# A four-layer graph network: mask pieces on one queue into eight buffers, and the first broadcast rows in memory of their own

## The chip, the cores and the metric

The kernel runs on one core of a Trainium2 chip. The metric is the device time of one launch in microseconds (us). The engines in the text are PE (TensorE, matrix products; PEld is its weight load), DVE (VectorE), ACT (ScalarE), POOL (GpSimd) and SP (SyncE, which only issues transfers). All transfers of the core run on 16 DMA engines; SP, ACT and POOL each issue into a queue of their own.

## The reference

Four graph layers run one after the other over N = 3327 nodes with 512 features, each added to its input and normalised over the features. The adjacency `adj` is an int32 matrix of 0 and 1, the same for all layers.

```python
# layers 0, 2 and 3: attention with H = 8, 8, 4 heads
Wh = h @ W                                # split into H heads
e = leaky_relu(f1[i] + f2[j], 0.2)        # f1, f2: two dot products of Wh with a
masked = where(adj > 0, e, -9e15)
attention = softmax(masked, axis=j)
h_prime = attention @ Wh                  # per head; layers 2 and 3: elu of it
# layer 1: mean over the first 64 neighbours of each node
keep = (adj > 0) & (cumsum(adj > 0, axis=1) <= 64)
xj = leaky_relu(mean over keep of X @ W_nb.T + b_nb)
xi = leaky_relu(X @ W_line.T + b_line)
out = xi + where(cnt > 0, xj, 0)
# around each layer
x = layernorm(x + layer(x, adj))
```

## The kernel before

Nodes are padded to 26 tiles of 128 (`NT`); a half (`HALF` = 13 tiles, `IW` = 1664 nodes) is what one attention pass covers as columns i.

**The mask.** The transposed adjacency is read once, in 104 pieces of 128 x 832 int32 (416 KB, `QW` = 832), each into a buffer `raw` (`mask_load`), and turned into an fp8 mask that stays in memory for all layers (`mask_set`, on DVE at L524 or on ACT at L523). `mask_steps` makes a list of steps: step k issues the load of piece k and sets the mask of piece k - lag. The pieces are in the order in which the attention needs them: first both quarters of the first half for all tiles in turn, then the third quarter for all tiles, then the fourth. The first 60 (`EARLY`) are issued in the projection of layer 0, from a pool of four buffers (`p_r`) with a lag of 3, two or three steps per tile, in turn from SP's and ACT's queue. The other 44 are `aside` steps of the attention, one per inner step, from two buffers (`rawp`) with a lag of 1; of those the ACT sets the ones whose number k has k % 5 in (1, 3).

**Projection of layer 0.** For each tile t, `project1` transposes the tile of x (four PE transposes, L253) and sums it (L256), and `project2` for the tile before makes 16 products into two PSUM banks (`pw`, L264); ACT copies the columns f1, f2 (`fc`, L268; `dc`, L265), DVE scales the result into `vt` (L270), and SP stores it to DRAM as `v` (L276). The tile of x is loaded by SP into one of three buffers. After tile 14 (`t == HALF + 1`), `prepare` makes the rows `r` of the first half (L298 to L314; four small stores to DRAM on SP) and `cut` splits columns into bf16 parts (L327 to L341). `mean` makes one more row of v after the last tile.

**Attention.** `attention` calls `unit` for two halves x four groups s of heads (`HS` = 2 heads each in layers 0 and 2, 1 in layer 3). A unit first loads for each of its heads the row `r` of this half, broadcast to 128 partitions (`rb`, L353, 832 KB, on POOL's queue, from a pool of `HS` + 1 buffers). Then for each of 26 tiles j it makes t = max(rb, qc) * mask on DVE (L396), a sigmoid y of t on ACT (L399), the products of t with the tile `vj` of v (`po`, PE L405; `vj` comes by SP, L391) and the denominators from y (`pd`, PE L365). In the first unit of layer 0, `prepare` and `cut` of the second half and the counts for layer 1 (`count_jobs`) run as background steps, in the second the small weight products of layers 2 and 3 (`attend`, PE L919).

**Layers 1 to 3.** Layer 1 (`sage`) projects all tiles into `zs` (two bf16 parts that stay in memory) and `zd`, then sums over the kept neighbours (`acc`, PE L728). Its last products are the start of layer 2, whose projection is done tile by tile as each tile of layer 1 is ready; after it `piece_columns` clears `sden` and `sm` on POOL (L245, L247), `cut` runs on DVE, and the attention of layer 2 begins. `third` does the same as layer 0 for layer 3, without mask pieces.

The order of instructions on each engine is that of the program as a scheduler has placed it; an engine runs its own list in order and waits at each instruction for what it needs. Pools hand out buffers; a pool that opens where another has been closed waits until that memory is free.

Of the kernel before, what the change touches and what calls it, by code (L numbers as in the profile page):

```python
# [7 lines left out]
F32 = mybir.dt.float32  # L8
# [10 lines left out]
P = 128  # L19
# [13 lines left out]
def kernel(  # L33
# [189 lines left out]
    class Layer:  # L223
        def __init__(self, li, H, elu):
            self.li, self.H, self.D, self.elu = li, H, F // H, elu
            self.HS = H // NS
            self.vd = dram.tile([NP, F], F32, name=f"v{li}")
            self.rd = dram.tile([H, NP], F32, name=f"r{li}")

# [29 lines left out]
        def project2(self, pool, bank, wsb, xT, t):  # L259
            H, D = self.H, self.D  # L260
            pw = [bank(e) for e in range(2)]
            for c in range(FC):
                for e in range(2):
                    nc.tensor.matmul(pw[e][:, :FW + H], xT[:, c, :], wsb[:, c, e, :], start=c == 0, stop=c == FC - 1)  # L264
            nc.scalar.activation(self.dc[:, t, :], pw[1][:, FW:FW + H], AF.Exp, scale=ALPHA)  # L265
            vt = pool.tile([P, H, D], F32, name="vt")
            for e in range(2):
                nc.scalar.copy(self.fc[:, t, e * H:(e + 1) * H], pw[e][:, FW:FW + H])  # L268
                hs = slice(e * H // 2, (e + 1) * H // 2)
                nc.vector.tensor_tensor(vt[:, hs, :], pw[e][:, :FW].rearrange("p (h d) -> p h d", d=D),  # L270
                                        self.dc[:, t, hs].rearrange("p (h e) -> p h e", e=1)
                                        .to_broadcast([P, H // 2, D]), op=ALU.mult)
            vv = vt.rearrange("p h d -> p (h d)")
            n = P if t < NT - 1 else LAST
            for a, z in _row_pieces(n):
                nc.sync.dma_start(out=self.vd[t * P + a:t * P + z, :], in_=vv[a:z, :])  # L276


        def mean(self, pool, bank, wsb):
# [62 lines left out]
                                            op0=ALU.mult)  # L342


        def unit(self, pools, half, s, background, aside, final=None, ending=None):
            H, D, HS = self.H, self.D, self.HS
            tp, yp, vp, rp, sp, po_p = pools
            i0 = half * IW
            heads = list(range(s * HS, (s + 1) * HS))
            rb = []  # L350
            for h in heads:
                r_ = rp.tile([P, IW], F32, name="rb")
                nc.gpsimd.dma_start(out=r_, in_=self.rd[h:h + 1, i0:i0 + IW].to_broadcast([P, IW]))  # L353
                rb.append(r_)
            po = [po_p.tile([P, 512], F32, name=f"po{c}") for c in range(4)]
            if s == 0:
                self.pd = [po_p.tile([P, 512], F32, name=f"pd{c}") for c in range(2)]
# [117 lines left out]

        def attention(self, extra=None, aside=(), later=None, final=None, ending=None):
            with tc.tile_pool(name="at_r", bufs=self.HS + 1, reuse_waits="tile") as rp, \
                    tc.tile_pool(name="at_t", bufs=3 * self.HS, reuse_waits="tile") as tp, \  # L480
                    tc.tile_pool(name="at_y", bufs=4 * self.HS - (self.li == 0), reuse_waits="tile") as yp, \
                    tc.tile_pool(name="at_v", bufs=4, reuse_waits="tile") as vp, \
                    tc.tile_pool(name="at_s", bufs=2, reuse_waits="tile") as sp, \
                    tc.tile_pool(name="at_po", bufs=1, space=PSUM, reuse_waits="tile") as po_p:
                pools = (tp, yp, vp, rp, sp, po_p)
                jobs = []
                aside = list(aside)
                for half in range(2):
                    for s in range(NS):
                        if extra:  # L490
# [12 lines left out]
    queue_ = [0]  # L503

    def mask_load(pool, t, q):
        n = P if t < NT - 1 else LAST
        i0 = q * QW
        w_ = min(QW, N - i0)
        raw = pool.tile([P, QW], I32, name="raw")
        queue_[0] ^= 1  # L510
        eng = (nc.sync, nc.scalar)[queue_[0]]
        for a, z in _row_pieces(n):
            eng.dma_start(out=raw[a:z, :w_], in_=adjT[t * P + a:t * P + z, i0:i0 + w_])
        return raw
# [9 lines left out]
        return nc.vector.tensor_scalar(dst, raw[:n, :w_], 0.0, None, op0=ALU.is_gt, saturate=False)  # L524


    def mask_steps(pool, pieces, lag, on_act, pinned):
        held = []

        def step(k):  # L530
            if k < len(pieces):
                held.append(mask_load(pool, *pieces[k]))
            if k >= lag:
                ins = mask_set(held[k - lag], *pieces[k - lag], on_act=(k - lag) in on_act)
                if pinned:
# [40 lines left out]
    def sage(first, first_pool, xin, prev, nxt, wsrc, dst):  # L576
# [3 lines left out]
        with tc.tile_pool(name="sg_z", bufs=1, reuse_waits="tile") as zp, \  # L580
# [11 lines left out]
                carry[b, t] = cy  # L592

            load_carry()
            zs = zp.tile([P, NT, 2, F], BF, name="zs")
            zd = dram.tile([NP, F], BF, name="zd")
            with tc.tile_pool(name="sa_w", bufs=1, reuse_waits="tile") as wp, \
                    tc.tile_pool(name="sa", bufs=2, reuse_waits="tile") as fp, \
# [15 lines left out]
                def step2(xt, xT, t):  # L614
# [6 lines left out]
                    nc.scalar.copy(zs[:, t, 0, :], pz)  # L621
                    r1 = sp.tile([P, F], F32, name="r1")
                    nc.vector.tensor_tensor(r1, pz, zs[:, t, 0, :], op=ALU.subtract)
                    nc.scalar.copy(zs[:, t, 1, :], r1)
                    z3 = sp.tile([P, F], BF, name="z3")
                    nc.vector.tensor_tensor(z3, r1, zs[:, t, 1, :], op=ALU.subtract)
# [19 lines left out]
            with tc.tile_pool(name="sb_w", bufs=1, reuse_waits="tile") as wp, \  # L646
# [71 lines left out]
                for b in range(len(blocks)):  # L718
# [3 lines left out]
                    for s in range(G):  # L722
                        acc = ps.tile([P, F], F32, name="acc", bufs=2)
                        for t in range(NT):
                            if b == 0 and len(kts) < NT:
                                kts.append(kept(0, len(kts)))
                            for c in range(3):
                                nc.tensor.matmul(acc, kts[t][:, s * P:(s + 1) * P],  # L728
                                                 zs[:, t, c, :] if c < 2 else zl[:, t, :],
                                                 start=t == 0 and c == 0, stop=t == NT - 1 and c == 2)  # L730
                            if not last and (len(ahead) < 10 and t % 2 == 1 and b > 0 if s == 0 else
                                             len(ahead) < min(NT, t + 11)):
# [20 lines left out]


    def third(first):
        with tc.tile_pool(name="col3", bufs=1) as cp:
            L3.columns(cp)
            L3.more_columns(cp)
            L3.piece_columns(cp)
            with tc.tile_pool(name="p_w", bufs=1, reuse_waits="tile") as wp, \  # L760
# [12 lines left out]
                for t0 in range(0, NT, 2):  # L773
                    ys, ahead = ahead, finish(fp, x2, L2, t0 + 2, 2) if t0 + 2 < NT else None
                    for s, y in enumerate(ys):
# [14 lines left out]
            with tc.tile_pool(name="f3", bufs=2) as fp, tc.tile_pool(name="f4", bufs=1) as gp:  # L790
# [60 lines left out]
                def final(s, q0, n, pt):  # L851
# [17 lines left out]
                L3.attention(lambda pool, half, s: [lambda: L3.prepare(fp, 1, "xr", 2), lambda: L3.cut(fp, 1, "e", 2)]  # L869
                             if (half, s) == (0, 0) else [], later=later, final=final)  # L870
                cut_ = min(8, HALF)
                for qs in (slice(0, cut_), slice(cut_, HALF)):
# [13 lines left out]

    fin0 = ExitStack()
    f0 = fin0.enter_context(tc.tile_pool(name="fin0", bufs=1, side="right"))
    with tc.tile_pool(name="col0", bufs=1) as cp, tc.tile_pool(name="raw", bufs=2) as rawp:
# [61 lines left out]
        def first_jobs(pool, half, s):  # L951
# [14 lines left out]

        pieces = pieces[EARLY:]
        ends = []
        L0.attention(first_jobs, mask_steps(rawp, pieces, 1, [k for k in range(len(pieces)) if k % 5 in (1, 3)], True),
                     ending=lambda: ends.extend(finish(f0, x, L0, 0, 2, 2)))  # L970

    with tc.tile_pool(name="col2", bufs=1) as cp:
        L2.columns(cp)
        L2.more_columns(cp)
        sage(ends, fin0, x, L0, L2, w2, x2)
        with tc.tile_pool(name="fin2", bufs=1) as f2:
            ends = []
            with tc.tile_pool(name="more2", bufs=1, reuse_waits="tile") as mp:
                L2.piece_columns(mp)
                L2.cut(mp, 0, "pc", 1)  # L980
                L2.attention(lambda pool, half, s: [lambda: L2.prepare(mp, 1, "rr", 1), lambda: L2.cut(mp, 1, "pc", 1)]
                             if (half, s) == (0, 0) else [],
                             ending=lambda: ends.extend(finish(f2, x2, L2, 0, 2, 2)))
            third(ends)
# [46 lines left out]
```

## Time and profile before

| | us |
|---|---|
| median of 3 runs | 3499.28 (3495.52 to 3499.89) |
| profiled execution | 3489.1 |
| its span in the profile | 3486.7 |

The profile page gives these busy times, as a share of the span.

| engine | busy us | share |
|---|---|---|
| PE | 3325.6 | 95% |
| DVE | 2694.9 | 77% |
| ACT | 2396.6 | 69% |
| POOL | 181.2 | 5% |

| group of the profile page | count | busy us | mean ns |
|---|---|---|---|
| DVE t L396, 128 x 1664 | 1040 | 1960.1 | 1947 |
| ACT y L399, 128 x 1664 | 1040 | 1771.7 | 1766 |
| PE po L405, 128 x 448 | 8320 | 1939.5 | 522 |
| PE pw L264, 128 x 264 | 1248 | 299.3 | 395 |
| DVE mask L524, 128 x 832 | 86 | 50.2 | 592 |
| POOL issue of rb L353 | 40 | 21.5 | 539 |

The shares are means over stages with different limits. The first projection takes the first 150 us of the span; the attention of layer 0 runs to 985 us, layer 1 to 1818, layer 2's attention from there to about 2620, layer 3's from 2761. In the profile's rows a name such as "raw<-in_adjT_dram" says that something waits for a transfer or an instruction that writes `raw` from the adjacency in DRAM. "DMA share" in a table of windows is the mean busy share of the 16 DMA engines, the last column what they moved in GB/s, and PEclk the clock that TensorE was granted.

### The profile page before, as it was taken

How to read it: one execution, taken by the hardware profiler on the slowest of the kernel's cores; microseconds unless marked ns; L12 is line 12 of the kernel's file. 1: busy time of each engine (PE TensorE's matmuls, PEld its weight loads, DVE VectorE, ACT ScalarE, POOL GpSimd, SP SyncE). 2: the span in 40 equal slices, each digit the busy share in tenths (PEclk: the TensorE clock that was granted, in tenths of full speed). 3: DMA queues.
4: the chain of work that ended last, by engine and by line, in shares of the span. 5: the costliest groups of instructions: out<-in, count | busy, mean ns of one | idle time of the engine just before them, and what ended most of it. 6: DMA issues, size and time to landing. Idle time of an engine off the chain costs nothing.

```text
span 3486.7 us, 48120 instructions
## 1 busy us (share of the span) xinstructions
PE 3325.6 (95%) x18873; PEld 1701.2 (49%) x18926; DVE 2694.9 (77%) x2759; ACT 2396.6 (69%) x2336; POOL 181.2 (5%) x289
## 2 busy tenths in 40 slices
PE   6899999999989999999998999999998999999997
PEld 5644444444444455555553444444446754555553
DVE  5599999999967644434439999999998756668886
ACT  1388989899953343433428999899998655558885
POOL 1000000000000111111110000000001000000000
PEclk9999999999999999999999999999999999999998
DMA  9535211101133432222221111111116511112211
GB/s 352 179 104 161 67 44 41 54 27 51 37 105 125 131 90 73 70 61 75 73 66 35 48 47 48 47 46 46 29 39 197 183 33 44 40 46 91 81 38 47
DMA packets 208452, 276.65 MB, mean 79 GB/s; under 512 B 19321, under 2 KB 140355, under 8 KB 208228
## 3 DMA queue, kind: packets, MB, share of 16 engines
q1 hardware_dynamic: 173622, 157.37, 14.1%
q0 software_dynamic: 22736, 89.80, 8.3%
q10 hardware_dynamic: 11870, 26.42, 2.4%
q8 instruction: 149, 2.44, 0.3%
q14 instruction: 75, 0.61, 0.1%
HBM read 204.92 MB, written 68.60 MB: 78 GB/s over the span
## 4 chain that ended last, share of the span: by engine, by line
PE 62%; issue 24%; DVE 6%; DMA 5%; ACT 3%; POOL 1%; POOLq 0%; DVEq 0%; SPq 0%; ACTq 0%
PE po L405 34%; PE acc L728 9%; PE pw L264 5%; PE pd L365 5%; DVE t L396 3%; PE pz L617 2%; PE pi L620 2%; DMA raw<-in_adjT_dram 2%; ACT y L399 1%; DMA cy<-ctd 1%; PE pt L429 1%; PE pk L696 1%; PE pt L253 1%; DVE kt L700 1%; PE pe L460 1%
## 5 line engine op out<-in xcount | busy, mean ns | idle before, releaser
L396 DVE SCALAR_TENSOR_TENSOR t<-rb,qc,mask 128x1664 f32<-128x1664 f32 x1040 | 1960.1, 1947 | 200.8 <-PE po L405 158.6
L399 ACT ACTIVATE y<-t,bi,sc 128x1664 fp8e4<-128x1664 f32 x1040 | 1771.7, 1766 | 341.4 <-PE pd L365 317.4
L405 PE MATMUL po<-t,vj 128*64 128x448 f32 (+3 forms) x8320 | 1939.5, 522 | 26.0 <-DVE t L396 24.6
L405 PEld LDWEIGHTS po<-t,vj 128*64 128x64 f32 (+1 forms) x8320 | 857.8, 148 | 977.7 <-issue 681.1
L728 PE MATMUL acc<-zs,kt 128*128 128x512 bf16 x1314 | 396.6, 381 | 1.9 <-issue 0.4
L264 PE MATMUL pw<-wsb,xT 128*128 128x264 f32 (+1 forms) x1248 | 299.3, 395 | 21.7 <-DVE vt L270 19.5
L688 ACT CAST pk<-cy 128x256 f32<-128x256 bf16 x338 | 124.0, 374 | 272.7 <-DVE kt L700 224.8
L728 PEld LDWEIGHTS <-kt 128*128 128x128 fp8e4 x2028 | 198.8, 98 | 229.6 <-issue 34.5
L264 PEld LDWEIGHTS pw<-wsb,xT 128*128 128x128 f32 x1248 | 238.9, 196 | 65.6 <-issue 18.8
L365 PE MATMUL pd<-y,sden 128*32 128x448 fp8e4 (+1 forms) x4160 | 259.8, 342 | 10.5 <-ACT y L399 10.5
L700 DVE SCALAR_TENSOR_TENSOR kt<-pk,mask 128x256 fp8e4<-128x256 f32 x338 | 140.9, 421 | 159.5 <-PE pk L696 158.9
L728 PE MATMUL acc<-zl,kt 128*128 128x512 bf16 x661 | 252.1, 381 | 1.1 <-DMA zl<-zd 0.5
L365 PEld LDWEIGHTS <-sden 128*32 128x32 bf16 x4160 | 117.8, 96 | 162.4 <-issue 139.8
L270 DVE TENSOR_TENSOR vt<-pw,dc 128x256 f32<-128x256 f32 x156 | 59.1, 418 | 98.1 <-ACT dc L265 93.5
L696 PE MATMUL pk<-mask,upto 128*128 128x256 fp8e4 x338 | 92.5, 274 | 21.1 <-ACT pk L688 20.0
L353 POOL DMA_DIRECT2D rb<-r x40 | 21.5, 539 | 1646.8 <-DVE t L396 1610.1
L268 ACT COPY fc<-pw 128x8 f32<-128x8 f32 (+1 forms) x156 | 22.8, 163 | 112.1 <-PE pw L264 101.8
L617 PE MATMUL pz<-wn,xT 128*128 128x512 f32 x208 | 95.0, 600 | 1.2 <-ACT xT L611 1.2
L620 PE MATMUL pi<-wl,xT 128*128 128x512 f32 x208 | 93.5, 592 | 0.0
L590 POOL DMA_DIRECT2D cy<-ctd x91 | 67.8, 745 | 400.2 <-ACT pk L688 273.5
L708 DVE SCALAR_TENSOR_TENSOR y<-acc,cnt,bnb 128x512 f32<-128x512 f32 x26 | 19.5, 751 | 85.1 <-PE acc L728 85.1
L524 DVE TENSOR_SCALAR mask<-raw 128x832 fp8e4<-128x832 int32 (+2 forms) x86 | 50.2, 592 | 45.0 <-DMA raw<-in_adjT_dram 44.4
(165 smaller groups left out, 1732.2 us busy)
## 6 DMA issues: line engine op xcount, KB each, us to landing
vj<-v SPq DMA_DIRECT2D x312, 128.0 KB
rb<-r POOLq DMA_DIRECT2D x40, 832.0 KB, 4.7
cy<-ctd POOLq DMA_DIRECT2D x78, 256.0 KB, 3.9
v<-vt SPq DMA_DIRECT2D x75, 256.0 KB
h<-hd SPq DMA_DIRECT2D x65, 256.0 KB
raw<-in_adjT_dram ACTq DMA_DIRECT2D x38, 416.0 KB
raw<-in_adjT_dram SPq DMA_DIRECT2D x37, 416.0 KB
hd<-hb SPq DMA_DIRECT2D x60, 256.0 KB
```

The lines of the kernel that those rows point to most:

```text
L264: nc.tensor.matmul(pw[e][:, :FW + H], xT[:, c, :], wsb[:, c, e, :], start=c == 0, stop=c == FC - 1)
L365: nc.tensor.matmul(pd[c][32 * kk:32 * kk + 32, :w_], lhsT, rhs, start=(kk, c) not in seen, skip_group_check=final is not None, stop=last a ...
L396: nc.vector.scalar_tensor_tensor(t, rb[k], self.qc[:, j, h:h + 1], mask[:, j, i0:i0 + IW], op0=ALU.max, op1=ALU.mult)
L399: nc.scalar.activation(y, t, AF.Sigmoid, bias=self.bi[:, j, h:h + 1], scale=self.sc[:, j, h:h + 1], saturate=False)
L405: nc.tensor.matmul(po[c][k * D:(k + 1) * D, :z - a_], vj[:, j % 2, k * D:(k + 1) * D], ts[k][:, a_:z], start=j == 0, stop=j == NT - 1)
L590: nc.gpsimd.dma_start(out=cy[:, :n, :], in_=ctd[t:t + n, b * GW:(b + 1) * GW] .rearrange("(o t) i -> o t i", o=1).to_broadcast([P, n, GW]))
L617: nc.tensor.matmul(pz, xT[:, c, :], wn[:, c, :], start=c == 0, stop=c == FC - 1)
L620: nc.tensor.matmul(pi, xT[:, c, :], wl[:, c, :], start=c == 0, stop=c == FC - 1)
L688: nc.scalar.copy(pks[k % 2], carry[b, t // 4 * 4][:, t % 4, :])
L696: nc.tensor.matmul(pk, upto, mask[:, t, i0:i0 + GW], start=False, stop=True, skip_group_check=True)
L700: nc.vector.scalar_tensor_tensor(kt, pk, NEIGHBOURS, mask[:, t, i0:i0 + GW], op0=ALU.is_le, op1=ALU.mult, saturate=False)
L728: nc.tensor.matmul(acc, kts[t][:, s * P:(s + 1) * P], zs[:, t, c, :] if c < 2 else zl[:, t, :], start=t == 0 and c == 0, stop=t == NT - 1 ...
```

## The change

There are four parts.

1. **Mask pieces.** `mask_load` takes its queue as an argument. The first four pieces go out on ACT's queue, all others on SP's, in the projection and in the attention. The early pool has 8 buffers in place of 4 and a lag of 5 in place of 3; 3 or 4 steps are issued per tile in place of 2 or 3; and `EARLY` is 88 in place of 60, so that 16 pieces are left for the attention.
2. **Transfers of the first projection.** The stores of v in layer 0 and the loads of x from tile 3 on are issued by POOL in place of SP.
3. **First rows.** The loads of `rb` become a method `rows`. For the first unit of each attention they are issued ahead of it: in layers 0 and 3 after `prepare` at tile 14 of the projection, in layer 2 ahead of `piece_columns`. The pool of the rows is opened outside of `attention`, so that it does not share memory with what runs before. Its number of buffers is the same as before (3, 3 and 2).
4. **Layout.** `zs` becomes two tiles of 13 node tiles each, and the pool `fin2` is placed on the other side of the memory.

```diff
-                nc.sync.dma_start(out=self.vd[t * P + a:t * P + z, :], in_=vv[a:z, :])
+                (nc.gpsimd if self.li == 0 else nc.sync).dma_start(out=self.vd[t * P + a:t * P + z, :], in_=vv[a:z, :])
...
+        def rows(self, rp, half, s):
+            rb = []
+            for h in range(s * self.HS, (s + 1) * self.HS):
+                r_ = rp.tile([P, IW], F32, name="rb")
+                nc.gpsimd.dma_start(out=r_, in_=self.rd[h:h + 1, half * IW:(half + 1) * IW].to_broadcast([P, IW]))
+                rb.append(r_)
+            return rb
...
-            rb = []
-            for h in heads:
-                r_ = rp.tile([P, IW], F32, name="rb")
-                nc.gpsimd.dma_start(out=r_, in_=self.rd[h:h + 1, i0:i0 + IW].to_broadcast([P, IW]))
-                rb.append(r_)
+            rb, self.first_rows = self.first_rows or self.rows(rp, half, s), None
...
-            with tc.tile_pool(name="at_r", bufs=self.HS + 1, reuse_waits="tile") as rp, \
-                    tc.tile_pool(name="at_t", bufs=3 * self.HS, reuse_waits="tile") as tp, \
+            with tc.tile_pool(name="at_t", bufs=3 * self.HS, reuse_waits="tile") as tp, \
...
-    queue_ = [0]
-
-    def mask_load(pool, t, q):
+    def mask_load(pool, t, q, eng):
...
-        queue_[0] ^= 1
-        eng = (nc.sync, nc.scalar)[queue_[0]]
...
-                held.append(mask_load(pool, *pieces[k]))
+                held.append(mask_load(pool, *pieces[k], nc.scalar if k < ahead else nc.sync))
...
-            zs = zp.tile([P, NT, 2, F], BF, name="zs")
+            zs_ = [zp.tile([P, HALF, 2, F], BF, name=f"zs{i}") for i in range(2)]
...
+        with tc.tile_pool(name="col3", bufs=1) as cp, tc.tile_pool(name="at_r3", bufs=2, reuse_waits="tile") as rp:
...
                             L3.prepare(pp, 0)
+                            L3.first_rows = L3.rows(rp, 0, 0)
                             L3.cut(pp, 0)
...
+    with tc.tile_pool(name="col0", bufs=1) as cp, tc.tile_pool(name="raw", bufs=2) as rawp, \
+            tc.tile_pool(name="at_r0", bufs=3, reuse_waits="tile") as rp:
...
-                tc.tile_pool(name="p_r", bufs=4, reuse_waits="tile") as rw0, \
+                tc.tile_pool(name="p_r", bufs=8, reuse_waits="tile") as rw0, \
...
-            EARLY = 2 * NT + 8
-            msteps = mask_steps(rw0, pieces[:EARLY], 3, (), False)
+            EARLY = 3 * NT + 10
+            msteps = mask_steps(rw0, pieces[:EARLY], 5, (), False, 4)
...
-                load_tile(xt, x, t, nc.sync)
+                load_tile(xt, x, t, nc.sync if t < 3 else nc.gpsimd)
...
-                for _ in range(3 if t % 5 < 2 else 2):
+                for _ in range(3 + t % 2):
...
                     L0.prepare(pp, 0)
+                    L0.first_rows = L0.rows(rp, 0, 0)
                     L0.cut(pp, 0)
...
-        with tc.tile_pool(name="fin2", bufs=1) as f2:
+        with tc.tile_pool(name="fin2", bufs=1, side="right") as f2:
             ends = []
-            with tc.tile_pool(name="more2", bufs=1, reuse_waits="tile") as mp:
+            with tc.tile_pool(name="at_r2", bufs=3, reuse_waits="tile") as rp, \
+                    tc.tile_pool(name="more2", bufs=1, reuse_waits="tile") as mp:
+                L2.first_rows = L2.rows(rp, 0, 0)
                 L2.piece_columns(mp)
```

More of the change, by code (lines that the diff above doesn't have):

```diff
@@ L226, in __init__ @@
             self.HS = H // NS
+            self.first_rows = None
             self.vd = dram.tile([NP, F], F32, name=f"v{li}")
@@ L473, in unit, with attention @@
             return jobs[:2] + [reciprocals] + jobs[2:]
-        def attention(self, extra=None, aside=(), later=None, final=None, ending=None):
-            with tc.tile_pool(name="at_r", bufs=self.HS + 1, reuse_waits="tile") as rp, \
-                    tc.tile_pool(name="at_t", bufs=3 * self.HS, reuse_waits="tile") as tp, \
+        def attention(self, rp, extra=None, aside=(), later=None, final=None, ending=None):
+            with tc.tile_pool(name="at_t", bufs=3 * self.HS, reuse_waits="tile") as tp, \
                     tc.tile_pool(name="at_y", bufs=4 * self.HS - (self.li == 0), reuse_waits="tile") as yp, \
@@ L524, in mask_set, with mask_steps @@
         return nc.vector.tensor_scalar(dst, raw[:n, :w_], 0.0, None, op0=ALU.is_gt, saturate=False)
-    def mask_steps(pool, pieces, lag, on_act, pinned):
+    def mask_steps(pool, pieces, lag, on_act, pinned, ahead=0):
         held = []
@@ L594, in sage, with zs @@
             load_carry()
-            zs = zp.tile([P, NT, 2, F], BF, name="zs")
+            zs_ = [zp.tile([P, HALF, 2, F], BF, name=f"zs{i}") for i in range(2)]
+            def zs(t, c):
+                return zs_[t // HALF][:, t % HALF, c, :]
             zd = dram.tile([NP, F], BF, name="zd")
@@ L620, in step2 @@
                         nc.tensor.matmul(pi, xT[:, c, :], wl[:, c, :], start=c == 0, stop=c == FC - 1)
-                    nc.scalar.copy(zs[:, t, 0, :], pz)
+                    nc.scalar.copy(zs(t, 0), pz)
                     r1 = sp.tile([P, F], F32, name="r1")
-                    nc.vector.tensor_tensor(r1, pz, zs[:, t, 0, :], op=ALU.subtract)
-                    nc.scalar.copy(zs[:, t, 1, :], r1)
+                    nc.vector.tensor_tensor(r1, pz, zs(t, 0), op=ALU.subtract)
+                    nc.scalar.copy(zs(t, 1), r1)
                     z3 = sp.tile([P, F], BF, name="z3")
-                    nc.vector.tensor_tensor(z3, r1, zs[:, t, 1, :], op=ALU.subtract)
+                    nc.vector.tensor_tensor(z3, r1, zs(t, 1), op=ALU.subtract)
                     nc.sync.dma_start(out=zd[t * P:(t + 1) * P, :], in_=z3)
@@ L728, in sage @@
                                 nc.tensor.matmul(acc, kts[t][:, s * P:(s + 1) * P],
-                                                 zs[:, t, c, :] if c < 2 else zl[:, t, :],
+                                                 zs(t, c) if c < 2 else zl[:, t, :],
                                                  start=t == 0 and c == 0, stop=t == NT - 1 and c == 2)
@@ L755, in third @@
     def third(first):
-        with tc.tile_pool(name="col3", bufs=1) as cp:
+        with tc.tile_pool(name="col3", bufs=1) as cp, tc.tile_pool(name="at_r3", bufs=2, reuse_waits="tile") as rp:
             L3.columns(cp)
@@ L867, in final @@
                             nc.vector.bn_aggr(out=mv[:, q, :], in_=st[:, q, :, :])
-                L3.attention(lambda pool, half, s: [lambda: L3.prepare(fp, 1, "xr", 2), lambda: L3.cut(fp, 1, "e", 2)]
+                L3.attention(rp, lambda pool, half, s: [lambda: L3.prepare(fp, 1, "xr", 2), lambda: L3.cut(fp, 1, "e", 2)]
                              if (half, s) == (0, 0) else [], later=later, final=final)
@@ L888 @@
     f0 = fin0.enter_context(tc.tile_pool(name="fin0", bufs=1, side="right"))
-    with tc.tile_pool(name="col0", bufs=1) as cp, tc.tile_pool(name="raw", bufs=2) as rawp:
+    with tc.tile_pool(name="col0", bufs=1) as cp, tc.tile_pool(name="raw", bufs=2) as rawp, \
+            tc.tile_pool(name="at_r0", bufs=3, reuse_waits="tile") as rp:
         L0.more_columns(cp)
@@ L968 @@
         ends = []
-        L0.attention(first_jobs, mask_steps(rawp, pieces, 1, [k for k in range(len(pieces)) if k % 5 in (1, 3)], True),
+        L0.attention(rp, first_jobs, mask_steps(rawp, pieces, 1, [k for k in range(len(pieces)) if k % 5 in (1, 3)], True),
                      ending=lambda: ends.extend(finish(f0, x, L0, 0, 2, 2)))
@@ L975 @@
         sage(ends, fin0, x, L0, L2, w2, x2)
-        with tc.tile_pool(name="fin2", bufs=1) as f2:
+        with tc.tile_pool(name="fin2", bufs=1, side="right") as f2:
             ends = []
-            with tc.tile_pool(name="more2", bufs=1, reuse_waits="tile") as mp:
+            with tc.tile_pool(name="at_r2", bufs=3, reuse_waits="tile") as rp, \
+                    tc.tile_pool(name="more2", bufs=1, reuse_waits="tile") as mp:
+                L2.first_rows = L2.rows(rp, 0, 0)
                 L2.piece_columns(mp)
                 L2.cut(mp, 0, "pc", 1)
-                L2.attention(lambda pool, half, s: [lambda: L2.prepare(mp, 1, "rr", 1), lambda: L2.cut(mp, 1, "pc", 1)]
+                L2.attention(rp, lambda pool, half, s: [lambda: L2.prepare(mp, 1, "rr", 1), lambda: L2.cut(mp, 1, "pc", 1)]
                              if (half, s) == (0, 0) else [],
```

## The prediction

> **What bounds the kernel now.** I read the windows of equal stages first, to see which resource is full in each stage, then the chain of waits inside the first projection and at the start of each attention, then shorter windows and the timeline for the bounds.
>
> ```profile
> core 0: us, PE busy (x) PEld busy (x) DVE busy (x) ACT busy (x) POOL busy (x), PEclk, DMA share, GB/s
> 0.00:100.00 100.00, 70.89 (x314) 59.34 (x315) 54.68 (x107) 13.72 (x57) 12.66 (x26) 0.97 0.99 350
> 100.00:164.00 64.00, 54.85 (x271) 45.42 (x269) 32.87 (x91) 17.82 (x61) 2.37 (x4) 0.95 0.47 159
> 164.00:273.00 109.00, 101.54 (x744) 42.93 (x745) 105.50 (x75) 90.01 (x61) 0.34 (x1) 0.97 0.37 108
> 273.00:384.00 111.00, 104.30 (x754) 50.82 (x750) 104.84 (x69) 95.89 (x68) 1.58 (x4) 0.97 0.45 134
> ...
> 489.00:587.00 98.00, 96.68 (x675) 43.79 (x673) 97.32 (x54) 91.03 (x61) 1.06 (x2) 1.00 0.14 44
> ```
>
> For 100 us the DMA engines are full (share 0.99) while TensorE (PE) is busy 71%: the projection is bound by bytes. From 100 to 164 us the DMA engines are half empty (0.47). In attention units 0 and 1 (164 to 273, 273 to 384) VectorE (DVE) is 97% and 94% busy and each takes 109 and 111 us, against 98 us for unit 3 (last line), which sets no mask and is 99% DVE. So there is free DMA time before the attention, and masks cost time inside it.
>
> ```profile
> 27.45 0.60 DVE mask L524
> 28.05 0.02 issue
> 28.07 6.43 DMA raw<-in_adjT_dram
> ...
> 35.15 6.33 DMA raw<-in_adjT_dram
> ```
>
> This is the chain in the projection (start, length, what): each tile stops 6 us for a `raw` piece, not for a computation. And where the attention starts:
>
> ```profile
> 156.16 0.58 issue
> 156.74 6.63 DMA rb<-r
> 163.37 0.03 issue
> 163.39 1.96 DVE t L396
> ```
>
> The chain there is the load of the broadcast rows `rb`. DVE has other work meanwhile: its idle time before the first two `t` is 2.51 and 0.69 us in the timeline, so the 6.63 us are mostly covered. At the two other attentions:
>
> ```profile
> 1823.97 0.04 DVE pc L327
> ...
> 1824.10 0.51 DVE vt L270
> 1824.62 0.03 DVE rest L328
> 1824.64 7.20 DMA v<-vt
> ...
> 2756.64 4.50 PE pw L264 x21
> 2761.14 1.87 DVE t L396
> ```
>
> In layer 2 a 7.20 us store wait leads, in layer 3 the last projection matmuls: neither start is set by `rb`.
>
> **The change, part by part.** One profiled execution gives the durations: it took 3489.1 us (span 3486.7). The median shown is 3499.28 us, 1.0029 times as much; I make the sum against 3489.1 and scale the result by 1.0029.
>
> (a) *Start of the first attention: +1.5 us, bounds -5.2 and +12.8.* Of the 104 pieces, 88 instead of 60 now come before the attention. A piece is 128 x 832 x 4 B = 0.426 MB, so 28 more are 11.9 MB. Before, 100 x 0.350 + 64 x 0.159 = 45.2 MB moved up to 164 us, of which two pieces for the attention (0.85 MB) and four `vj` loads of 0.128 MB (0.5 MB) will now come later. That leaves 45.2 - 1.35 + 11.9 = 55.8 MB before the last early piece. At the 350 GB/s of the full window, 159.4 us. Per tile that is 3.5 pieces plus a 0.26 MB load of x and store of v, 2.02 MB or 5.8 us, against 4.0 us of PE (`pw` x16 3.56 plus `pt` 0.44) and 3.6 us of DVE (3.5 x 0.594 + 2 x 0.42 + 0.69): DMA sets the pace to the last tile, and the cover for the extra sets is the DVE's own waiting. After the last piece come its set (0.6 us) and, in the changed order of DVE, seven small instructions of the second `cut` (about 3 us), then two `t` of 1.95: 159.4 + 0.6 + 3.0 + 3.9 = 166.9. Before, the second `t` ended at 163.39 + 1.96 = 165.35. The `rb` wait is gone from this, since its three 0.85 MB loads are inside the 55.8 MB (they were inside the 45.2 MB too). The bounds are the slowest and fastest ten microseconds with DMA full:
>
> ```profile
> 20.00:30.00 10.00, 10.00 (x42) 8.46 (x42) 6.12 (x13) 1.48 (x5) 0.00 (x0) 1.00 0.99 327
> ...
> 70.00:80.00 10.00, 5.88 (x30) 4.73 (x29) 6.32 (x14) 1.85 (x9) 0.00 (x0) 1.00 1.03 385
> ```
>
> At 327 GB/s the last piece is there at 170.6, +12.8 in the end. At 385 it is there at 145, and then the old chain decides without its `rb` step: 156.2 + 3.9 = 160.1, -5.2.
>
> The Trainium skill ("DMA: Bandwidth & Descriptors", Specifications) gives about 358 GB/s as the limit of memory for one core; the trace has 353, 373 and 385 over ten microseconds, so the row decides. By the page alone the last piece would be there at 156 us and this term would be -2.
>
> (b) *Fewer mask sets in units 0 and 1: -9.4 us, bounds -9.5 and 0.* Of the 44 late pieces DVE set 26 and ACT 18; of the 16 left, DVE sets 10 and ACT 6. All 16 fall in unit 0. So unit 0 loses 6 x 0.59 = 3.5 us of DVE and unit 1 10 x 0.59 = 5.9. DVE is the full engine there, so both count. ACT's 12 sets of 0.976 us count for nothing: it is busy 90 of 109 us. Zero is the bound if PE (101.5 and 104.3 us busy) holds the units up instead. The sets that move into the projection cost nothing there, as (a) counts them under the DMA pace; without that cover, 16.6 us of DVE (28 x 0.592).
>
> (c) *Waits for transfers in units 0 and 1: -2 us.* The chain has 4.90 us for `raw` at 253.31, 4.47 for `wt` at 327.49 and 3.30 for `wt` at 354.29. The first happens in unit 0, where pieces stay; the others stand beside 10 pieces that leave, but a `wt` load also waits for its one buffer, and that stays. PE's busy time is the floor: 109 + 111 - 101.5 - 104.3 = 14.2 us is all that (b) and (c) can give together. The other bound is 0.
>
> (d) *Layer 2: +2 us, bounds 0 and +5.8.* The rows are issued before the memsets, but did not lead. What changes is DVE's order: the first `cut` ran from 1823.97 to 1829.8 while the projection's last stores landed, and is now queued behind `rc`, which needs the last tile's `fc` (1830.65). So 5.8 us of DVE leave an idle gap and fall where `t` starts. In return `t` goes ahead of the second `cut`: the first `t` moves only from 1837.51 to 1838.8 (+1.3), and DVE has 2.08 us of waiting soon after (at 1855.26) that absorbs part. I take +2.
>
> (e) *Layer 3: -1.5 us, bounds -4 and +1.* With rows already there, `t` goes one tile earlier in DVE's order and the first sigmoids too. The start before holds a PE stall from the `x21` group's end at 2761.14 to 2776.56 with table switches of 1.28 us each on ACT; a tile (4.0 us) is the most that can come forward, one switch the most that is lost.
>
> (f) *At nothing.* The queue moves: 25 v stores and 23 x loads now issue on POOL at 0.53 us each, 25 us of an engine that is idle from 20 to 100 us; the cover is that idleness, and the price without it 1.1 us a tile. Behind POOL's wait for the `r` rows stand the stores and x loads of two to three tiles; x is loaded two tiles ahead (11.5 us), and the `r` write stands behind at most eight pieces (8 x 0.426 / 0.350 = 9.7 us), so PE just about keeps x. SP's `vj` loads now wait for the end of the projection, two microseconds while the first `t` run. The split `zs` changes nothing: its first cast waits for its own matmul (1012.4).
>
> One sentence of the same page, in "SWDGE vs HWDGE vs iDMA", speaks against the move to POOL: the software queue's rings lie in on-chip memory that DVE can lock POOL out of. The trace has the `rb` issues at 0.528 us in 480 to 600 us with DVE 99% busy, as fast as elsewhere, and I add nothing; the page gives no time for a sum.
>
> Sum: 1.5 - 9.4 - 2 + 2 - 1.5 = -9.4 us; 3479.7, times 1.0029 = **3490 us**.
>
> **Rivals.**
>
> *1. The projection grows by more than the units shrink (slower).* Its place is the DMA engines from 100 us on, where `rb`, x and v sit on one queue and all `raw` on another, and POOL's stalls let bytes run dry. The trace's own sign is the stretch in which early pieces mixed with `r` traffic:
>
> ```profile
> 95.00:110.00 15.00, 14.51 (x68) 11.70 (x69) 11.74 (x37) 4.77 (x18) 0.00 (x0) 0.89 0.91 309
> ```
>
> At 309 GB/s over all 55.8 MB the last piece is there at 180.6: (a) becomes +22.7 and the sum +11.8, so 3511 us. Against it: PE was full in that stretch, so the demand had ended. It decides from 317 GB/s down (last piece at 176 us); between 331 and 317 the sum is 0 to 0.2%.
>
> *2. More than the sum (faster).* The DMA engines hold 373 to 385, the start comes at its floor (-5.2), and the units fall to PE's busy time (-14.2): with d and e as above -18.9, so 3480 us. For it: two of eight windows reach it. Against: 350 is the mean of all.
>
> *3. The sets that leave are replaced by other idle time, no change.* PE or the counts that hang on the last pieces hold units 0 and 1: (b) is 0 and the sum 0, 3499 us. For it: unit 4 takes 103 us without mask sets, so not all of the excess is masks. Against: DVE busy 105.5 of 109.
>
> **How the numbers follow.** About 0.2% (7 us) is what can be told from no change. Forecast 3490, own range 3483 to 3497: 0.40 (faster 0.27, same 0.13). Rival 1: 0.25 (slower 0.22, same 0.03). Rival 2: 0.20, all faster. Rival 3: 0.15 (same 0.10, slower 0.05). Faster 0.47, same 0.26, slower 0.27. The low end is the floors of (a), (b), (c) and (e) with (d) at 0: -5.2 - 14.2 - 4 = -23.4, 3476; the high end rival 1, 3511.
>
> **What would show it.** (a): DMA share near 1 to about 160 us, and the second `t` ending near 167; later than 175 and rival 1 is true. (b): units 0 and 1 near 105 and 103 us. (c): the `wt` waits shorter. (d): `cut` behind `rc`, first `t` 1.3 us later after the last `acc`. (e): PE's stall before the long `po` run shorter by 1 to 2 us. A projection with DMA share below 0.9 before its last tile would break the pace of (a) and the forecast with it.

## The result and the profile after

| | before | after |
|---|---|---|
| median | 3497.4 us (4 runs, 3491.38 to 3499.89) | 3477.0 us (4 runs, 3474.25 to 3483.24) |
| ratio | 1 | 0.9947 (95% interval 0.9927 to 0.9966) |
| profiled execution | 3489.1 us | 3476.2 us |

The change makes the kernel 0.5% faster. The medians differ by 20.4 us, the two profiled executions by 12.9. What follows compares profiled executions, at points that both have in their timelines. The "second `t`" is the second of the DVE instructions `t` with which the attention begins. "Rows of unit n" is the `rb` load that POOL issues when the last `t` of unit n - 1 with its first head frees a buffer, and so marks the end of unit n - 1.

| us | before | after | difference |
|---|---|---|---|
| end of the second `t` | 165.35 | 159.81 | -5.5 |
| rows of unit 1 | 272.66 | 266.99 | -5.7 |
| rows of unit 2 | 383.69 | 367.21 | -16.5 |
| rows of unit 7, layer 0 | 886.36 | 869.93 | -16.4 |
| last `y` of layer 1 | 1818.07 | 1799.61 | -18.5 |
| rows of unit 7, layer 2 | 2528.44 | 2512.71 | -15.7 |
| end of the last DVE instruction | 3478.21 | 3464.83 | -13.4 |

All of the gain is there when unit 2 of layer 0 begins. The windows of the changed kernel, with the same columns as those of the prediction (span, then busy time of PE, PEld, DVE, ACT and POOL, the granted clock, DMA share, GB/s):

```profile
0.00:100.00 100.00, 83.95 (x412) 72.00 (x413) 63.00 (x136) 20.90 (x80) 35.09 (x61) 1.00 0.99 370
100.00:164.00 64.00, 45.01 (x185) 33.86 (x184) 43.56 (x91) 14.59 (x41) 11.87 (x20) 0.84 0.85 319
```

The DMA engines are as full as before in the first 100 us (0.99), but move 370 GB/s in place of 350, and PE is busy 84 us in place of 71. From 100 to 164 us they are now used, 0.85 in place of 0.47. Between 20 and 80 us the difference is larger:

```profile
20.00:80.00 60.00, 46.81 (x211) 38.53 (x211) 34.67 (x69) 8.09 (x38) 0.00 (x0) 0.97 1.00 355
```

is the kernel before, and

```profile
20.00:80.00 60.00, 57.71 (x280) 49.38 (x281) 40.51 (x80) 12.56 (x50) 17.74 (x28) 1.00 1.03 404
```

the changed one: 404 GB/s, and PE busy 57.7 of 60 us. The DMA engines are full there too, but PE's waits for DVE's `vt` in this stretch fall from 13.2 to 2.3 us: it hardly stops any more. DVE's timeline at the start of the attention in the changed kernel (start, length, line, what, and in brackets the idle time before it):

```profile
155.79 0.37 DVE L342 TENSOR_SCALAR sm<-pc 128x156 bf16<-128x156 bf16 x1
156.01 7.52 DVE L402 SCALAR_TENSOR_TENSOR t<-rb,qc,mask 128x1664 f32<-128x1664 f32 x4
...
175.16 5.68 DVE L402 SCALAR_TENSOR_TENSOR t<-rb,qc,mask 128x1664 f32<-128x1664 f32 x3 [3.47 <-PE po L411]
```

`t` follows `cut` without a gap: no wait for rows. The gap of 3.47 us for `po` comes later; the kernel before has one of 2.92 us at 179.44, there put down to ACT's `y`. The clock granted to PE is 0.58 in 156 to 166 us and 0.50 in 160.7 to 170.7 before. Unit 1, before and then after:

```profile
272.60:383.60 111.00, 104.30 (x750) 51.04 (x750) 104.84 (x69) 95.89 (x67) 1.61 (x3) 0.97 0.45 134
```

```profile
267.00:367.20 100.20, 99.92 (x755) 47.47 (x751) 98.04 (x56) 88.18 (x58) 1.65 (x3) 1.00 0.20 63
```

DVE has 6.8 us less work (13 set instructions, 7.7 us, are gone), and its idle time falls from 6.2 to 2.2 us; PE is now full. The chain's waits for `wt` (weights that `attend` reads), 4.47 and 3.30 us before, are gone from it; what is left of PE's waits for `wt` is 0.6 us each.

### The profile page after: what moved, and what is told of

The parts are those of the page before. It is cut to its first block, busy times and chain, and to the rows that moved or that the text cites. A ratio compares the mean times of both kernels' runs of the same rounds, so it can differ in the third digit from the quotient of the medians.

```text
span 3474.4 us, 48117 instructions
## 1 busy us (share of the span) xinstructions
PE 3320.6 (96%) x18873; PEld 1700.4 (49%) x18926; DVE 2699.8 (78%) x2771; ACT 2387.0 (69%) x2324; POOL 213.3 (6%) x340
## 4 chain that ended last, share of the span: by engine, by line
PE 59%; issue 27%; DVE 6%; DMA 5%; ACT 2%; POOL 1%; ACTq 0%; POOLq 0%; SPq 0%; DVEq 0%
PE po L411 33%; PE acc L734 9%; PE pd L371 4%; PE pw L265 4%; DVE t L402 3%; DMA raw<-in_adjT_dram 3%; PE pz L623 3%; PE pi L626 2%; PE pt L435 1%; ACT y L405 1%; DMA cy<-ctd 1%; PE pk L702 1%; DVE kt L706 1%; PE pe L466 1%; PE pt L254 1%
## 5 line engine op out<-in xcount | busy, mean ns | idle before, releaser
L526 DVE TENSOR_SCALAR mask<-raw 128x832 fp8e4<-128x832 int32 (+2 forms) x98 | 58.4, 603 | 51.0 <-DMA raw<-in_adjT_dram 50.7
```

## The experiments

Times within a kernel are from its profile. The same table serves all of them; ratios are against the kernel before, on the same chip. "Per busy time" is the rate over 20 to 80 us divided by the DMA share. Each row is one execution; the stretch from unit 2 to unit 7, whose code is the same in all, takes 501.2 to 503.4 us, so differences of two or three microseconds between rows are not read.

| kernel | GB/s, share, per busy time | first `t` | rows of unit 1 | of unit 2 | of unit 7 | ratio |
|---|---|---|---|---|---|---|
| before | 355, 1.00, 355 | 160.75 | 272.66 | 383.69 | 886.36 | 1 |
| after | 404, 1.03, 392 | 156.01 | 266.99 | 367.21 | 869.93 | 0.9947 (0.9927-0.9966) |
| 1: x, v on SP | 304, 0.87, 349 | 194.57 | 304.11 | 404.30 | 905.80 | 1.0063 (1.0048-1.0078) |
| 2: pieces on two queues | 394, 1.03, 383 | 175.19 | 284.71 | 385.06 | 887.10 | 0.9999 (0.9989-1.0008) |
| 3: four buffers | 372, 1.00, 372 | 164.33 | 276.46 | 376.81 | 879.18 | 0.9984 (0.9973-0.9996) |
| 4: before, 88 early | 350, 0.99, 354 | 176.11 | 286.81 | 387.22 | 888.79 | 0.9997 (0.9987-1.0006) |
| 5: no rows ahead | 406, 1.03, 394 | 150.24 | 260.47 | 360.78 | 863.09 | 0.9938 (0.9916-0.9960) |
| 6: rows ahead in layer 0 only, r on ACT | 407, 1.03, 395 | 153.10 | 263.34 | 363.50 | 865.96 | 0.9937 (0.9920-0.9954) |
| 7: x, v on ACT | 381, 1.01, 377 | 157.19 | 267.50 | 367.57 | 869.89 | 0.9950 (0.9936-0.9965) |
| 8: 60 early | 400, 1.03, 388 | 144.38 | 256.13 | 363.36 | 865.22 | 0.9946 (0.9929-0.9962) |
| 9: 60 early, no rows ahead | 402, 1.03, 390 | 145.21 | 259.29 | 368.61 | 869.79 | 0.9939 (0.9923-0.9956) |
| 10: no rows ahead, r on ACT | 406, 1.03, 394 | 151.50 | 261.92 | 362.33 | 865.75 | 0.9933 (0.9920-0.9947) |
| 11: as 10, 74 early | 407, 1.03, 395 | 144.06 | 257.44 | 362.66 | 864.58 | 0.9938 (0.9925-0.9950) |
| 12: before, queues alone | 357, 0.97, 368 | 151.13 | 264.39 | 374.32 | 877.00 | 0.9977 (0.9965-0.9988) |

**1 to 4: which part raises the rate.** The profile after had shown more bytes per busy microsecond, which no step of the prediction holds. Three parts of the change could be the cause; one run takes back each, and the fourth makes the other half of the change alone.

Run 1, on the changed kernel:

```diff
-                (nc.gpsimd if self.li == 0 else nc.sync).dma_start(out=self.vd[...], in_=vv[a:z, :])
+                nc.sync.dma_start(out=self.vd[...], in_=vv[a:z, :])
-                load_tile(xt, x, t, nc.sync if t < 3 else nc.gpsimd)
+                load_tile(xt, x, t, nc.sync)
```

> The changed kernel with the x loads and the layer-0 v stores back on SP. Theory A (packets): the transfers of x and v are what made the DMA engines faster, since on POOL's queue they go in packets of about 4 KB and on SP's of 2 KB; the rate over 20 to 80 us falls from 404 to about 355 GB/s, the first t moves from 156.0 to 165-172 us, and the time rises by 10 to 15 us to 3487-3492. Rival B (one queue for the pieces) and rival C (eight buffers): the rate stays near 404, the first t stays within 4 us of 156, the time within 5 us of 3477.

It was far worse than either theory: slower than the kernel before (1.0063), first `t` 38.6 us later than in the changed kernel. The rate per busy time falls to 349, as theory A said, but the DMA engines are also idle for 13% of the time, which nobody had forecast. The chain of waits in this run:

```profile
70.54 0.33 SPq L277
70.87 0.04 issue
70.91 0.51 SPq L515
71.42 0.06 issue
71.48 1.52 SPq L515
73.00 0.04 issue
73.04 0.02 SPq L126
73.06 0.05 issue
73.11 4.68 DMA xt<-in_x_dram
```

SP issues a store of v (L277), then pieces (L515), and only then the load of x (L126) that PE waits for. What holds SP up is the store, which waits until DVE has made `vt`. SP's largest group of waits in 20 to 190 us (us in total, times, longest):

```profile
SPq L277 <- DVE vt L271: 89.0, 24, 9.9
```

With two smaller entries, SP stood 98.4 us at the stores of v, and 2.0 us at the pieces. PE waited 41.2 us for `xt` in the same time. The pieces stand behind the same stores, which fits the DMA engines running dry.

Run 2, on the changed kernel:

```diff
-                held.append(mask_load(pool, *pieces[k], nc.scalar if k < ahead else nc.sync))
+                held.append(mask_load(pool, *pieces[k], nc.scalar if k < ahead or k % 2 else nc.sync))
```

> The changed kernel with every second piece on ACT's queue again (x and v stay on POOL's, eight buffers). Theory A: the rate over 20 to 80 us stays at 395 GB/s or more and the time within 5 us of 3477, apart from what ACT loses by waiting at its own issues. Rival B: the rate falls to about 355 GB/s, the first t comes at 165-172 us, the time is 3487-3492.

The rate stays at 394 GB/s, so rival B falls: one queue for the pieces does not make the DMA engines faster. Yet the first `t` is 19 us later, and 17 us remain at unit 7. What is left of the theory is "what ACT loses by waiting". ACT's waits in 20 to 150 us (engine and line, for what; us in total, times, longest), first in the kernel before:

```profile
ACT dc L265 <- DVE mask L524: 43.4, 10, 6.2
ACT fc L268 <- PE pw L264: 24.9, 11, 3.4
```

then in the changed kernel, where no wait for `mask` is among them (the two longest),

```profile
ACT fc L269 <- PE pw L265: 75.1, 24, 9.4
ACT xT L256 <- PE pt L254: 17.1, 23, 12.0
```

and in run 2:

```profile
ACT dc L266 <- DVE mask L526: 28.4, 8, 5.0
...
ACT fc L269 <- DVE mask L526: 14.3, 3, 5.0
ACT xT L256 <- DVE mask L526: 10.1, 4, 2.8
```

`dc` reads nothing that a mask set writes. It waits because ACT stands at the issue of a piece ahead of it, and that piece waits until DVE has emptied its buffer. In the kernel before, ACT's timeline has the issue and, right behind it, `dc` after 5.41 us of idle time:

```profile
57.75 0.34 ACTq L513 DMA_DIRECT2D raw<-in_adjT_dram  x1
58.13 0.18 ACT L265 ACTIVATE dc<-pw 128x8 f32<-128x8 f32 x1 [5.41 <-DVE mask L524]
```

As DVE's `vt` needs `dc`, and PE needs the bank that `vt` frees, the whole tile then goes at the pace of the pieces. With the pieces on SP (all but the first four), ACT waits for no mask set, and 98.6 of its 110.9 us of waiting are for PE.

Run 3, on the changed kernel: `bufs=8` of the early pool back to 4, and the lag from 5 to 3.

> The changed kernel with 4 buffers and a lag of 3 for the early pieces. Theory A: the rate over 20 to 80 us stays at 390 GB/s or more; only the stretch around the r writes (80 to 100 us) loses a little more, the first t comes 0 to 6 us later, time 3477-3483. Rival C: with four pieces in flight the rate falls to about 355 GB/s, the first t comes at 165-172 us, the time is 3487-3492.

Between the two: 372 GB/s over 20 to 80 us, and unit 7 9.3 us later. Eight buffers (with the longer lag that goes with them) matter, and not only around the r writes.

Run 4, on the kernel before: `EARLY = 3 * NT + 10`, and `3 + t % 2` steps per tile.

> The kernel before with 88 early pieces and 3.5 of them per tile, nothing else changed. All theories: the rate stays at about 355 GB/s, so the last early set comes at 160-168 us and the rows are loaded behind it; the second t ends at 170-178 us in place of 165.4, unit 1 falls by about 10 us, and the time is 3493-3501. If the number of early pieces alone were the gain, it would be 3480-3487.

As expected by all, the rate is 350 GB/s and unit 1 10.6 us shorter. The second `t` ends at 180.9 us, 2.9 us beyond the forecast's range. The later start and the shorter unit cancel (0.9997). Moving 28 pieces is worth nothing at the rate of the kernel before.

**5 to 8: the rows, the r writes, the kind of queue, the number of pieces.** Run 5, on the changed kernel (and likewise in layers 2 and 3, with the pool opened in `attention` as before):

```diff
-                    L0.first_rows = L0.rows(rp, 0, 0)
...
-        L0.attention(rp, ...
+        L0.attention(None, ...
```

> The changed kernel with all three pools of the rows inside the attention again and no rows issued ahead; queues, buffers and early pieces stay. Read by stage. Layer 0: if the rows of their own memory are worth something, the first t waits for rows that are issued only when the projection's memory is free, and starts 3 to 8 us later than 156.0 (rival: nothing, as the rows were hidden behind other work before, at most 2 us). Layer 2: from the last y of layer 1 (L714 in the changed kernel) to the first row load of unit 1 it took 117.7 before and 119.9 after; theory: 117.7 again (rival: 119.9, if something else of the change costs it). Layer 3: the projection is 4 to 8 us faster without the rows' transfers among its own, and the attention's start 4 us slower; net 0 to 4 us faster.

The expectation for layer 0 had the wrong sign: the first `t` comes 5.8 us earlier without the rows ahead. DVE's timeline shows the wait that they avoid:

```profile
150.24 1.95 DVE L402 SCALAR_TENSOR_TENSOR t<-rb,qc,mask 128x1664 f32<-128x1664 f32 x1 [1.95 <-DMA rb<-r]
152.74 13.13 DVE L402 SCALAR_TENSOR_TENSOR t<-rb,qc,mask 128x1664 f32<-128x1664 f32 x7 [0.55 <-DMA rb<-r]
```

2.5 us of idle time. What they cost stands in the windows of 100 to 140 us, first with rows ahead (the changed kernel), then without (this run):

```profile
100.00:140.00 40.00, 30.46 (x133) 24.66 (x132) 21.87 (x44) 6.63 (x27) 9.00 (x15) 0.91 1.03 388
```

```profile
100.00:140.00 40.00, 36.06 (x168) 29.56 (x168) 26.95 (x57) 7.14 (x32) 10.04 (x15) 1.00 1.03 392
```

The DMA engines are full in both, and PE gets through 168 matrix instructions in place of 133. The rows are 2.56 MB, 6.2 us at 410 GB/s, which other transfers of a stage that is bound by bytes then lack; that this is what they cost is argued from these windows, and runs 8 and 9 below fit it. The sum is -5.1 us for the end of the second `t` (154.69 against 159.81). In layer 2 neither number of the expectation came: from the last `y` to the rows of unit 1 it took 121.0 us, but 116.8 in runs 10 and 11, which have the same layer 2, so this stretch tells nothing of the rows; layer 3 is told of below.

Run 6 keeps the rows ahead in layer 0 alone, and issues the r writes of the first half by ACT:

```diff
-                nc.sync.dma_start(out=self.rd[...], in_=rr[:, :n * P])
+                (nc.scalar if self.li == 0 and half == 0 else nc.sync).dma_start(out=self.rd[...], in_=rr[:, :n * P])
```

> The changed kernel with the rows of layers 2 and 3 as before the change, and the four r writes of the first half of layer 0 issued on ACT's queue in place of SP's. Theory: SP stood behind those writes, so that the rate fell to 311 GB/s in 80 to 100 us; now it is 380 or more there, and the first t comes at 151-155 in place of 156.0. Layers 2 and 3 gain 2 and 0 to 4 us. Time 3468-3475. Rival: the fall of the rate comes from the row and r traffic itself; then the first t stays at 156 and the time is 3472-3477.

The rate in 80 to 100 us rises from 311 to 372 GB/s, and the first `t` comes 2.9 us earlier: part of that stretch's fall was SP standing behind the writes. The rate of 380 that the theory had was not reached. The time, 3469.9 us, is in the theory's range and below the rival's, but the kernel before took 3492.0 us there in place of 3497.4, so the time does not separate them.

Run 7, on the changed kernel: `nc.gpsimd` becomes `nc.scalar` in the two lines that run 1's diff takes away.

> The changed kernel with the x loads and v stores of layer 0 on ACT's queue in place of POOL's. It tells packets from order. Theory A (packets): on a hardware queue of their own the transfers of x and v still go in 2 KB packets, and the bytes per busy time of the DMA engines stay at about 350 GB/s over 20 to 80 us (rate divided by busy share), as with x and v on SP. Rival D (a queue of their own, no matter of which kind): 385 GB/s or more. Time: under A 3485-3495, under D 3475-3485, since ACT waits at its own stores.

Run 7 settles theory A, which run 1 could not. In 40 to 80 us x and v go in packets of 1.8 KB on average on ACT's queue (2418 packets for 4.43 MB) against 3.3 KB on POOL's (1517 for 4.97 MB), and the rate there is 408 GB/s against 412. Over 20 to 80 us it is 381 GB/s (377 per busy time), below the forecast of rival D, because it starts slowly (356 in 20 to 50 us, 406 in 50 to 80). So small packets are not the cause. With x and v on a queue without pieces all runs with eight buffers have 377 to 395 GB/s per busy time, and those with four 368 to 372; with x and v among the pieces it is 349 with eight and 354 to 355 with four. That the mixture itself makes the DMA engines slower is not shown. In run 1 SP also stood at the stores of v, so that less may have been under way, and the kernel before, with its mixed queue and four buffers, reaches the rate of the changed one for eight microseconds:

```profile
64.00:72.00 8.00, 6.63 (x32) 5.37 (x30) 4.35 (x9) 1.59 (x8) 0.00 (x0) 0.93 1.04 412
```

In turn the changed kernel falls to 311 GB/s at a share of 0.94 in 80 to 100 us, 331 per busy time, with its queues as they are. What sets the bytes per busy time stays open.

Run 8: `EARLY = 2 * NT + 8` in the changed kernel.

> The changed kernel with 60 early pieces in place of 88. Theory: the projection is no longer short of bytes, the first t comes at 147-152 us (PE's own time plus the tail), but units 0 and 1 take 111 us each as in the kernel before; so 9 to 11 us are lost in unit 1 and 4 to 9 won at the start: 3475-3485. If the early pieces are the whole gain, 3490-3497.

It is as fast as the changed kernel (0.9946 against 0.9947) with none of the 28 pieces moved, so they are not the gain. The first `t`, at 144.4 us, is 11.6 us earlier and earlier than forecast; unit 1 is only 7.0 us longer (107.2 us against 100.2; 111.0 before).

**9 to 12: combinations.** Run 9 is run 5 with 60 pieces, run 10 run 5 with run 6's r writes, run 11 the same with 74 pieces; run 12 is the kernel before with the two lines of the changed kernel that run 1's diff takes away, and `eng = nc.sync` for every piece.

> The changed kernel with 60 early pieces and no rows issued ahead in any layer. In the run without rows the start of the attention was bound by bytes and won 3.3 us by leaving the rows out; in the run with 60 pieces it was bound by TensorE. Theory: with 60 pieces the rows ahead are worth something, because nothing else stands in the way: the first t comes 1 to 4 us later than the 144.4 of the run with 60 pieces and rows, the rows of unit 7 are issued at 862-868, and the time is 3467-3474, no better than without rows at 88. Rival: rows ahead cost in any case (POOL's queue waits for them); first t at 140-144, unit 7 at 857-862, time 3462-3467.

Run 9: the first `t` is 0.8 us later where 1 to 4 were forecast, unit 7 1.8 us beyond its range, the time (3473.46) inside. At 60 pieces, where bytes no longer bind (DMA share 0.54 in 100 to 140 us of run 8), leaving the rows out costs 4.6 us at unit 7; at 88 it saves 6.8. Of the 4.6 us only 0.8 are there at the first `t`, and the rest, in units 0 and 1, is not explained. The rival's start and unit 7 did not come. The ratios, over the whole kernel, don't separate the two (0.9939 and 0.9946).

> The changed kernel without rows issued ahead, and with the r writes of the first half of layer 0 on ACT's queue. Theory: both gains add, as one is fewer bytes and one a stall of SP's queue: the rate in 80 to 100 us is 400 or more in place of 333, the first t comes at 146-149 in place of 150.2, unit 7's rows at 859-862, time 3464-3468. Rival: TensorE is the bound by then (it is busy 1.00 up to 140 us in the run without rows), and nothing more comes: unit 7 at 863, time as in the run without rows.

Run 10: the theory falls, with 357 GB/s in 80 to 100 us, first `t` at 151.5, unit 7 at 865.75. The two gains don't add. Against run 6, which has the r writes on ACT and the rows ahead, leaving the rows out brings 1.6 us at the first `t` and 0.2 at unit 7, so the 6.8 us of run 5 are not the price of the rows alone.

> As the run before in this list, with 74 early pieces. Theory: 14 pieces fewer take 6.0 MB or 15 us off the DMA engines, so the start is TensorE's: first t at 143-147; 14 pieces in units 0 and 1 cost 8 of them on DVE, 5 us. The two cancel: unit 7's rows at 858-863, within 3 us of the run with 88. Rival: the start does not move (it is TensorE's already at 88), so 74 loses 3-6 us.

Run 11: the start is PE's, as forecast (144.06), and unit 7 comes within 1.2 us of run 10, though both later than expected.

> The kernel before with two edits alone: the x loads and v stores of layer 0 on POOL's queue, all pieces on SP's. Four buffers, a lag of 3, 60 pieces and the rows stay as before. Theory: the queues are most of the gain, since ACT no longer waits at pieces' issues and SP's queue is no longer mixed: the projection's tiles take less than 5 us, the last early set comes by 95-100 us in place of 110.6, the first t by 150-156 in place of 160.8, time 3480-3488. Rival: without the eight buffers nothing comes (four buffers cost 9.3 us at unit 7 in the changed kernel): time 3488-3495.

Run 12 lies in between: 0.9977, first `t` at 151.1, unit 7 9.4 us earlier than before. The sets did not all come as early as forecast (three stand at 107 to 109 us). The queues alone give a good half of the 16.4 us at unit 7; the rest comes only with the other parts, of which the buffers (run 3, 9.3 us) are the one whose own run shows a gain there.

No version is shown to be faster than the changed kernel. Run 10 has the lowest ratio, 0.9933 (0.9920 to 0.9947), and the intervals of runs 5 to 11 all overlap with that of the changed kernel (0.9927 to 0.9966). At unit 7 of the profiles run 5 is 6.8 us ahead.

## Why the prediction was half right

The sign was right. The time, 3477.0 us, lies below the forecast's own range (3483 to 3497) and 1 us inside the whole range, whose low end was 3476. The size, -9.4 us in the sum, was -13.4 at the end of DVE's work in the profiles and -20.4 between the medians. That the sum came as near as it did is partly luck: its first term had the wrong sign, its largest cause stood "at nothing", and the terms for the units were right only together. By its own steps:

- **(a), start of the attention: +1.5 forecast, -5.5 measured**, past the lower bound of -5.2. The step that failed is "At the 350 GB/s of the full window". I took the mean rate of full DMA engines for a property of the chip, and the fastest ten microseconds (385) for its limit. But eight microseconds of the same trace had 412 (run 7 above), and the change moved 404 over 20 to 80 us (416 in its best ten microseconds). In the runs the rate over 20 to 80 us went with what shared a queue and with how many pieces were under way: 372 with four buffers, 304 (349 per busy time) with x and v back among the pieces. At 404 the 55.8 MB take 138 us. The last early set came at 153.5, later than that, because the first 20 us moved 328 GB/s, 80 to 100 us 311 and 130 to 153.5 us 324.
- **(f), "at nothing", was the largest part.** I priced the move of x and v as issue time on POOL. Taken back, it costs 35.9 us at unit 7; pieces back on ACT's queue cost 17.2. Neither SP's stand at the stores of v nor ACT's at the pieces was in the sum. The wait of ACT was in the profile before, 43.4 us, and I passed over it, as the chain showed only the transfers behind it. What I feared of POOL's queue (rows, stores and x loads in one line) did not show: in 20 to 155 us of the changed kernel POOL waited 1.0 us for the r rows, and PE for no tile of x.
- **(b) and (c): -11.4 forecast together, -10.9 measured** between the second `t` and the rows of unit 2. The division was off: unit 0 fell by 0.1 us, not 3.5, unit 1 by 10.8. The kernel before had only 12 of its DVE sets between the first `t` and the end of unit 0 and 13 in unit 1, where I had counted 16 and 10 by the program's order. The waits for `wt` went almost altogether.
- **(d), layer 2: +2 forecast, +2.7 measured; (e), layer 3: -1.5 forecast, +2.4 measured.** Neither is settled. From the last `y` of layer 1 to unit 7 of layer 2 it is 710.4 us before and 710.2 in run 4, whose layer 2 is the same, but 714.1 in run 12, which has the same code too; the changed kernel has 713.1, and the five runs with its layer 2 (1, 2, 3, 7 and 8) have 710.2 to 711.9. From there to the end the kernel before has 949.8, run 4 952.1 and run 12 961.4, all with the same code; the changed kernel has 952.1, run 5 without rows ahead 950.3. What was read as a mechanism in DVE's order is there (`cut` stands behind `rc`, which waits 5.71 us for `fc`), but its price cannot be told from such differences. No run takes back the layout (part 4 of the change): from unit 7 of layer 0 to the last `y` of layer 1 the changed kernel has 929.7 us and the three kernels with the old layout 928.4 to 931.9, so no effect of it is visible.

```profile
1813.57 0.26 DVE L299 TENSOR_SCALAR rc<-fc 128x104 f32<-128x104 f32 x1 [5.71 <-ACT fc L269]
1813.75 0.39 DVE L328 CAST pc<-dc 128x104 bf16<-128x104 f32 x1
```

Rival 2 (3480 us) was nearest to the result, and for part of its reason: a rate above 350. Its other part, units 0 and 1 at PE's busy time, held for unit 1 alone. Rival 1 lost, though its rate of 309 GB/s around the r writes did come (311 in 80 to 100 us), for 20 us only, and run 4 shows it at work in the kernel before; what decided was whether the queues were changed with the pieces. Rival 3 did not occur. The figure of the Trainium skill ("DMA: Bandwidth & Descriptors", Specifications) of about 358 GB/s for one core, which it works out as half of what two cores share, was no bound for this kernel on one core: 404 GB/s over 60 us. The warning in "SWDGE vs HWDGE vs iDMA", that DVE in its 2-port mode locks POOL out of the memory in which POOL's queue has its rings, had no visible effect. The stores of v on POOL's queue took 0.545 us to issue in the median of 20 to 100 us (1.305 at most), and x and v on ACT's queue were no faster (0.9950 against 0.9947). No run shows whether DVE was in that mode.

## What to carry to other kernels

Before costing a transfer-bound stage by its mean rate, look at shorter windows for the rate that it can reach, and ask what stands ahead of each transfer in its queue. A load that the next computation needs, put behind a store that waits for a result, is late (run 1), and a compute engine that issues loads which wait for buffers stands still with them (run 2). A transfer that is brought forward into a stage that is bound by bytes can cost more there than its own wait: 5.8 us at the first `t` for 2.5 us of waiting in run 5, though 1.6 where the r writes were on ACT. Where bytes were free (runs 8 and 9) it cost nothing at the first `t`. And look for waits of an engine on something that it does not read: here they showed a queue in front of it.

## What was not expected of the hardware

DMA engines that are full by their busy share can differ by 14% in what they move: 355 GB/s at a share of 1.00 over 20 to 80 us of the kernel before, 404 at 1.03 in the changed one. Within the kernel before, ten-microsecond windows with a share of 0.98 or more go from 327 to 385. The granted clock of PE falls in the first ten microseconds of the first attention in every one of the fourteen profiles, to 0.50 (before) at the lowest, 0.58 in the changed kernel and 0.74 at the highest (run 3), after 5.7 to 12.2 us in which PE ran no matrix product.
